# Four graph layers on one core: the adjacency's transpose by block loads and a VectorE transpose, and layer 2's last product kept in PSUM

## The chip, the cores and the metric

The kernel runs on one core of one Trainium2 chip. The core has five engines that run side by side, each through its own queue and in order: TensorE (PE, with its weight loads as PEld), VectorE (DVE), ScalarE (ACT), GpSimd (POOL) and SyncE (SP, which here issues nearly all transfers). [...] The metric is the device time of one execution in microseconds (us); lower is better. A line number such as L997 is a line of the kernel before.

## The reference

The input is x, 64 graphs of 256 nodes with 256 features, and adj, a 256 x 256 matrix of weights for each graph. Four layers follow each other, each as x = layernorm(x + layer(x, adj)). Layer 0 is a recurrence over the nodes. The change lies in layers 1 to 3:

```python
# layer 1: normalized adjacency times a linear map
degree = adj.sum(-1); d = degree ** -0.5            # 0 where the degree is 0
out1 = relu((adj * d[:, :, None] * d[:, None, :]) @ (x @ W.T + b))
# layer 2: attention with one head, masked by adj
att = softmax(scores * adj - 9e15 * (1 - adj), axis=2)
out2 = relu((att @ v) @ Wo + bo)
# layer 3: attention with 8 heads of 32 features
scores = where(adj > 0, q @ k.T / sqrt(32), -9e15)
out3 = (softmax(scores) @ v) @ Wo + bo
```

## The kernel before, in words

`_recurrence` computes layer 0 node by node, for all graphs at once. `_layers` then does layers 1 to 3 graph by graph. Each graph is an object of class `Graph`, and each of its methods is one step. Rows and columns of a 256 x 256 matrix lie as [128 partitions, 2 halves, 256].

The order of work is written out by hand. `ROUND` (L1246) lists the steps of one round, and the loop at L1257 runs rounds t = -1 to 66. In one round five graphs are at work, each in another part of its way: L (graph t+1) adds the residual of layer 0, takes degrees and prepares adj; A (graph t) is in layer 1; B (t-1) in layer 2; C (t-2) and E (t-3) in layer 3. The schedule is manual, so every engine runs its part of the steps in the order of this list. A round begins with graph t+2's loads. A graph's loads are thus issued about two rounds ahead of their use; SP also has the two stores of a round in its queue (L1162 and L1242).

These steps matter for the change:

- `load` (L1030): three transfers of 256 KB from SP: xin (x), ad (adj, in its own layout) and y (layer 0's result).
- `adT` (L1065), the step L.adT near the end of a round. PE transposes ad by four 128 x 128 transposes against an identity into one PSUM bank (`flipped`, L982). ACT copies it out in two halves, scaled by the degrees' roots: adT, which layer 1 uses one round later (`g`, L1086). DVE makes neg3 from the same bank: 0 where the transposed adj is above 0, and -9e15 elsewhere. Layer 3 adds neg3 to its transposed scores (L1190).
- `xT` (L1076): PE transposes the normalized x of a graph, and ACT copies it to SBUF. The next round begins with A.xT.1 and B.xT.2, right behind L.adT.
- `s3` (L1171): layer 3's scores for four heads; DVE adds neg3 (L1190), ACT takes the exponential (L1191), and POOL adds the two halves of each head's result to p3s (L1193), from which PE makes the softmax's sums.
- `o3` (L1197): PE multiplies p3s by ones (L1207) and p by v (L1216). In the program it stands behind the two xT; behind it comes `qk2` (L1100), PE's product of the weights with B's xT.
- `f2` (L1141), the end of layer 2. PE's product pm lies in PSUM; DVE scales it by 1/sums and adds a bias row, half by half, into an SBUF tile f (L1145), and then does y = max(f, 0) + y (L1149).

The PSUM banks with the tag "mm" (L966) are four, handed round among all products and transposes of these steps.

Of the kernel before, what the change touches and what calls it, by code (L numbers as in the profile page):

```python
# [9 lines left out]
F32 = mybir.dt.float32  # L10
BF16 = mybir.dt.bfloat16
AF = mybir.ActivationFunctionType
ALU = mybir.AluOpType
AX = mybir.AxisListType

NEG = 9000000000000000.0
# [3 lines left out]
P = 128  # L20
# [891 lines left out]
def _layers(tc, ident, Hd, Yd, x, adj, weights, out):  # L912
# [8 lines left out]
    nc = tc.nc  # L921
    nat, W2, W3, b1_r, b2_r, b3_r, cols = weights
# [6 lines left out]
    with ExitStack() as ctx:  # L929
# [9 lines left out]
        io = ctx.enter_context(tc.tile_pool(name="l_io", bufs=3))  # L939
# [26 lines left out]
        def bank(name, shape=(P, 2, D)):  # L966
            return ps.tile(list(shape), F32, tag="mm", name=name, bufs=4)

        for c in range(2):
            pt = bank(f"w1_{c}", (P, 2, P))  # L970
# [11 lines left out]
        def flipped(src, t):  # L982

            pt = bank(f"tr_{t}")
            for a in range(2):
                for c in range(2):
                    nc.tensor.transpose(
                        pt[:, a, c * P:(c + 1) * P], src[:, c, a * P:(a + 1) * P], ident
                    )
            return pt  # L990

        def product(lhsT, rhs, t):

            pm = bank(f"mm_{t}")
            for c in range(2):
                for k in range(2):
                    nc.tensor.matmul(  # L997
                        pm[:, c, :], lhsT[:, k, c * P:(c + 1) * P], rhs[:, k, :],
                        start=(k == 0), stop=(k == 1),
                    )  # L1000
            return pm

        def new(tag, t, bufs=2, shape=(P, 2, D)):
            return work.tile(list(shape), F32, tag=tag, name=f"{tag}_{t}", bufs=bufs)
# [17 lines left out]
        class Graph:  # L1022
# [7 lines left out]
            def load(self):  # L1030
                b = self.b
                self.xin = io.tile([P, 2, D], F32, tag="xin", name=f"xin_{b}")
                nc.sync.dma_start(self.xin, x[b].rearrange("(c p) d -> p c d", p=P))
                self.ad = io.tile([P, 2, N], F32, tag="ad", name=f"ad_{b}", bufs=4)
                nc.sync.dma_start(self.ad, adj[b].rearrange("(c p) m -> p c m", p=P))
                self.y = io.tile([P, 2, D], F32, tag="y", name=f"y_{b}", bufs=7)
                nc.sync.dma_start(self.y, Hd[:, b, :].rearrange("(c p) d -> p c d", p=P))

# [24 lines left out]
                nc.vector.tensor_mul(self.dis, self.dis, self.some)  # L1063

            def adT(self):  # L1065
                pt = flipped(self.ad, f"ad_{self.b}")
                self.adT_sb = new("adT", self.b)
                for c in range(2):
                    nc.scalar.activation(
                        self.adT_sb[:, c, :], pt[:, c, :], AF.Copy, scale=self.dis[:, c:c + 1]  # L1070
                    )

                self.neg3 = new("neg3", self.b, 4)
                nc.vector.tensor_scalar(self.neg3, pt, 0.0, -NEG, ALU.is_le, ALU.mult)

            def xT(self, l):  # L1076
                pt = flipped(self.y, f"x{l}_{self.b}")
# [62 lines left out]

            def f2(self):  # L1141
                pm = product(self.pT2_sb, self.w2_sb, f"2f_{self.b}")
                f = new("f2", self.b)
                for c in range(2):
                    nc.vector.scalar_tensor_tensor(  # L1145
                        f[:, c, :], pm[:, c, :], self.sums2[:, c:c + 1], b2_r,
                        ALU.mult, ALU.add,
                    )
                nc.vector.scalar_tensor_tensor(self.y, f, 0.0, self.y, ALU.max, ALU.add)  # L1149


            def qk3(self, s):
# [104 lines left out]
        for t in range(-1, B + 3):  # L1257
            if 0 <= t + 2 < B:
                graphs[t + 2].load()
            for step in ROUND:  # L1260
                who, name, *args = step.split(".")
                b = t - "LABCE".index(who) + 1
# [213 lines left out]
```

## Time and profile before

| what | value |
|---|---|
| median of 3 runs | 3432.68 us (3432.17 to 3434.24) |
| the profiled execution | 3433.69 us |
| its span, first to last instruction | 3431.9 us |
| granted TensorE clock over the span | 0.980 |
| first ad load of layers 1 to 3 | at 1525.41 us |
| chain that ended last, by engine | PE 73%, DMA 9%, DVE 6%, SP's queue 3%, POOL 3%, ACT 2% |

The first 1524 us of the span are layer 0; the rest is layers 1 to 3. Busy time in the second part, 1600 to 3300 us, is the steady part of the rounds. The timeline gives start, length, engine, line, operation, out<-in, shapes and count; names there leave out numbers, so tr_ad is the bank of adj's transpose, mm the product of xT with weights, and neg stands for neg2 and neg3. In the slices of the page, each digit is a fortieth of the span, in tenths of busy time.

### The profile page before, as it was taken

Reading aid. Unit: us, or ns where it says so; the run is one execution under the profiler, and the core shown is the slowest. Engines: PE = TensorE matmul, PEld = TensorE weight load, DVE = VectorE, ACT = ScalarE, POOL = GpSimd, SP = SyncE. Lnnn points to the kernel's source line nnn. Section 1 sums busy time; section 2 is a strip of 40 time slices with the busy share of each in tenths; the row PEclk is TensorE's granted clock in tenths of the full one; section 3 lists DMA queues with packets and bytes.
Section 4 is the critical chain, followed back from the end, with each engine's and each line's share of the span. In section 5 each row is a group of like instructions: output and inputs, shape, how many; then the busy total and the mean of one; then the engine's idle time right before and its main releaser. Section 6 shows DMA issues by size and latency. Waiting matters only on the chain.

```text
span 3431.9 us, 79587 instructions
## 1 busy us (share of the span) xinstructions
PE 3219.7 (94%) x29350; PEld 2339.7 (68%) x29350; DVE 2480.2 (72%) x7061; ACT 1827.7 (53%) x4754; POOL 1871.0 (55%) x2165
## 2 busy tenths in 40 slices
PE   5799999999889998978999999999999999999997
PEld 4565555555445555547888888888888888888885
DVE  3476777766567777755888888888888888888875
ACT  0254454444444444435666666666666666666664
POOL 2376777676667777733444444444444444444443
PEclk8999999999999999999999999999999999999998
DMA  9756675788777575230111111111111111111100
GB/s 301 226 159 143 164 188 155 168 188 211 186 185 173 146 183 157 60 97 22 47 47 47 47 47 47 47 47 47 47 47 47 47 47 47 47 47 47 47 29 19
DMA packets 389341, 347.83 MB, mean 101 GB/s; under 512 B 107356, under 2 KB 355304, under 8 KB 383720
## 3 DMA queue, kind: packets, MB, share of 16 engines
q1 hardware_dynamic: 371256, 325.82, 35.3%
q10 hardware_dynamic: 17696, 16.91, 1.5%
q8 instruction: 234, 3.83, 0.5%
q14 instruction: 155, 1.27, 0.1%
HBM read 224.01 MB, written 99.61 MB: 94 GB/s over the span
## 4 chain that ended last, share of the span: by engine, by line
PE 73%; DMA 9%; DVE 6%; SPq 3%; POOL 3%; issue 3%; ACT 2%; ACTq 0%; POOLq 0%; DVEq 0%
PE mm L997 13%; PE rc L604 5%; PE rc L596 4%; PE s L1181 4%; PE mm_2f L997 3%; DVE ACC L629 3%; PE mm_3v L997 3%; PE mm_t L997 3%; PE mm_3f L997 3%; PE mm_2v L997 3%; PE mm_g L997 3%; PE mm_2s L997 3%; PE mm_2w L997 3%; PE o L1216 3%; PE late L520 3%
## 5 line engine op out<-in xcount | busy, mean ns | idle before, releaser
L629 DVE SCALAR_TENSOR_TENSOR ACC<-keep,S,ACC 128x128 f32<-128x128 f32 x1712 | 481.3, 344 | 256.5 <-ACT hs L647 228.1
L1193 POOL TENSOR_TENSOR p3s<-p 128x256 f32<-128x256 f32 x512 | 386.8, 786 | 366.8 <-ACT p L1191 366.5
L997 PE MATMUL mm<-xT,weights 128*128 128x256 f32 x2048 | 481.9, 383 | 2.8 <-ACT xT L1079 2.8
L997 PEld LDWEIGHTS mm<-xT,weights 128*128 128x128 f32 x2048 | 384.9, 190 | 79.3 <-issue 25.5
L1190 DVE TENSOR_TENSOR p<-s,neg 128x512 f32<-128x512 f32 x512 | 317.6, 682 | 115.3 <-PE s L1181 115.3
L666 POOL TENSOR_TENSOR ACC<-ACC,far 128x384 f32<-128x384 f32 (+1 forms) x313 | 372.6, 1190 | 24.6
L662 POOL TENSOR_TENSOR far<-hs,S 128x384 f32<-128x384 f32 (+1 forms) x313 | 304.2, 972 | 4.7
L961 ACT ACTIVATE y<-y,shift,rstd 128x256 f32<-128x256 f32 x512 | 273.4, 599 | 48.1 <-DVE shift L959 44.4
L1191 ACT ACTIVATE p<-p 128x512 f32<-128x512 f32 x512 | 295.3, 628 | 1.9 <-DVE p L1190 1.6
L803 POOL TENSOR_TENSOR ready<-ACC,dinv 128x128 f32<-128x128 f32 x255 | 101.7, 399 | 325.8 <-DVE ACC L629 325.8
L596 PE MATMUL rc<-WxT,xqT 128*64 128x256 f32 x2048 | 268.1, 382 | 0.6 <-issue 0.6
L1104 ACT ACTIVATE qk<-mm,weights 128x256 f32<-128x256 f32 x256 | 107.3, 470 | 269.6 <-PE mm L997 269.6
L613 ACT COPY xpT<-xpT_ps 128x128 f32<-128x128 f32 x256 | 68.1, 266 | 302.5 <-PE xpT_ps L611 302.5
L1093 POOL TENSOR_TENSOR y<-y,g 128x512 f32<-128x512 f32 x64 | 81.0, 1265 | 266.2 <-issue 266.2
L604 PE MATMUL rc<-WhT,rT 128*64 128x128 f32 x2048 | 170.2, 287 | 58.0 <-DVE rT L826 56.0
L1230 DVE RECIPROCAL rT<-o 128x256 f32<-128x256 f32 x128 | 223.7, 1748 | 0.3 <-PE o L1207 0.2
L953 POOL TENSOR_TENSOR rstd<-rstd,mhalf 128x2 f32<-128x2 f32 x256 | 173.5, 695 | 83.2 <-DVE rstd L952 81.5
L949 DVE BATCH_NORM_STATS2 st<-y 128x6 f32<-128x256 f32 x512 | 208.8, 408 | 10.5 <-POOL y L1093 9.8
L604 PEld LDWEIGHTS rc<-WhT,rT 128*64 128x64 f32 x2048 | 107.8, 137 | 158.1 <-DVE rT L826 137.0
L1058 POOL TENSOR_TENSOR dis<-dis,mhalf 128x2 f32<-128x2 f32 x64 | 44.8, 700 | 277.5 <-DVE dis L1057 260.7
L604 PE MATMUL rc<-WhT,xpT 128*64 128x128 f32 x2048 | 170.5, 288 | 26.7 <-ACT xpT L613 25.4
L604 PEld LDWEIGHTS rc<-WhT,xpT 128*64 128x64 f32 x2048 | 107.9, 137 | 115.3 <-ACT xpT L613 64.9
(161 smaller groups left out, 7378.5 us busy)
## 6 DMA issues: line engine op xcount, KB each, us to landing
xX<-in_x_dram ACTq DMA_DIRECT2D x16, 1024.0 KB
Us<-xu SPq DMA_DIRECT2D x64, 256.0 KB
xq<-in_x_dram SPq DMA_DIRECT2D x64, 256.0 KB
ACC<-Us SPq DMA_DIRECT2D x32, 512.0 KB
Es<-eu SPq DMA_DIRECT2D x64, 256.0 KB
early_sb<-Es SPq DMA_DIRECT2D x32, 512.0 KB
xin<-in_x_dram SPq DMA_DIRECT2D x64, 256.0 KB
ad<-in_adj_dram SPq DMA_DIRECT2D x64, 256.0 KB
```

The source lines that it names most:

```text
L596: nc.tensor.matmul(G[o * B:(o + 1) * B], xqT[a, i // 2][:, i % 2, kc, h * B:(h + 1) * B], WxT[:, kc, o, gates], start=False, stop=False, s ...
L604: nc.tensor.matmul(G[o * B:(o + 1) * B], hT[:, kc * B:(kc + 1) * B], WhT[:, kc, o, g], start=False, stop=(kc == 1), skip_group_check=True,)
L629: nc.vector.scalar_tensor_tensor(acc[:, 0, :], keep[:, j % 2, :], s, acc[:, 0, :], ALU.mult, ALU.add)
L662: nc.gpsimd.tensor_mul(tmp[:, 0:count, :], hs.unsqueeze(1).to_broadcast(shape), s.unsqueeze(2).to_broadcast(shape),)
L666: nc.gpsimd.tensor_add(acc, acc, tmp[:, 0:count, :])
L949: nc.vector.bn_stats(st, y[:, c, :])
L961: nc.scalar.activation(y[:, c, :], y[:, c, :], AF.Identity, bias=shift[:, c:c + 1], scale=rstd[:, c:c + 1],)
L997: nc.tensor.matmul(pm[:, c, :], lhsT[:, k, c * P:(c + 1) * P], rhs[:, k, :], start=(k == 0), stop=(k == 1),)
L1190: nc.vector.tensor_add(p, s_ps[i], self.neg3)
L1191: nc.scalar.activation(p, p, AF.Exp, scale=ISQ)
L1193: nc.gpsimd.tensor_add(both, p[:, 0, :], p[:, 1, :])
L1230: nc.vector.reciprocal(rT, o_ps[:, 1, :])
```

## The change

adT no longer goes through PE and PSUM. SP loads adj a second time, in 32 x 32 blocks: az has, on partition 32 j + r, for each half a of the columns, the rows r of eight row blocks i, with the 32 columns that begin at 128 a + 32 j. One DVE transpose then turns every 32 x 32 block in place, which puts the blocks where the whole transpose has them. ad itself is still loaded, since degrees and layer 2's mask use it. Each graph thus has eight more transfers, each of 256 pieces of 128 bytes, issued between ad and y.

ACT now reads the transpose from SBUF for adT, and so does DVE for neg3. In f2, DVE writes its scaled product back into the product's own PSUM bank, and the last operation reads it from there; the SBUF tile f is gone. The order in `ROUND` is as before.

```diff
@@ load
                 nc.sync.dma_start(self.ad, adj[b].rearrange("(c p) m -> p c m", p=P))
+                self.az = io.tile([P, 2, 8, 32], F32, tag="az", name=f"az_{b}", bufs=3)
+                for j in range(4):
+                    for a in range(2):
+                        at = a * P + j * 32
+                        nc.sync.dma_start(
+                            self.az[j * 32:(j + 1) * 32, a],
+                            adj[b, :, at:at + 32].rearrange("(i r) c -> r i c", r=32),
+                        )
                 self.y = io.tile([P, 2, D], F32, tag="y", name=f"y_{b}", bufs=7)
@@ adT
-                pt = flipped(self.ad, f"ad_{self.b}")
+                turned = new("adTr", self.b)
+                nc.vector.transpose(
+                    turned.rearrange("p a m -> p (a m)"), self.az.rearrange("p a i c -> p (a i c)")
+                )
                 self.adT_sb = new("adT", self.b)
                 for c in range(2):
                     nc.scalar.activation(
-                        self.adT_sb[:, c, :], pt[:, c, :], AF.Copy, scale=self.dis[:, c:c + 1]
+                        self.adT_sb[:, c, :], turned[:, c, :], AF.Copy, scale=self.dis[:, c:c + 1]
                     )
                 self.neg3 = new("neg3", self.b, 4)
-                nc.vector.tensor_scalar(self.neg3, pt, 0.0, -NEG, ALU.is_le, ALU.mult)
+                nc.vector.tensor_scalar(self.neg3, turned, 0.0, -NEG, ALU.is_le, ALU.mult)
@@ f2
-                f = new("f2", self.b)
                 for c in range(2):
                     nc.vector.scalar_tensor_tensor(
-                        f[:, c, :], pm[:, c, :], self.sums2[:, c:c + 1], b2_r,
+                        pm[:, c, :], pm[:, c, :], self.sums2[:, c:c + 1], b2_r,
                         ALU.mult, ALU.add,
                     )
-                nc.vector.scalar_tensor_tensor(self.y, f, 0.0, self.y, ALU.max, ALU.add)
+                nc.vector.scalar_tensor_tensor(self.y, pm, 0.0, self.y, ALU.max, ALU.add)
```

## Prediction

> **What bounds the kernel now.** I read four views, in this order. First the page: busy time by engine and the slices of the span.
>
> ```profile
> PE 3219.7 (94%) x29350; PEld 2339.7 (68%) x29350; DVE 2480.2 (72%) x7061; ACT 1827.7 (53%) x4754; POOL 1871.0 (55%) x2165
> PE   5799999999889998978999999999999999999997
> DVE  3476777766567777755888888888888888888875
> ```
>
> The change touches only the last 22 or so of the 40 slices, where TensorE (PE) is at 9. The busy time in stretches says how full it is there (columns: stretch, its length, then busy time of PE, PEld, DVE, ACT, POOL, the granted clock, DMA share, GB/s):
>
> ```profile
> 1600.00:3300.00 1700.00, 1699.83 (x11557) 1372.32 (x11556) 1368.34 (x3359) 1082.66 (x2356) 810.45 (x1002) 1.00 0.14 46
> ```
>
> PE has no idle time on the page and runs at full clock; VectorE (DVE) is at 80%, ScalarE (ACT) at 64%. Rounds repeat every 28.83 us (the same step starts at 2207.25 and at 2236.08 in the chain of waits). This invites the sum "four transposes fewer, so much faster". The chain of waits, for one round, shows where they lie (start, length, what):
>
> ```profile
> 2207.25 1.92 PE mm_2f L997 x8
> 2209.17 0.44 PE tr_ad L987 x4
> 2209.61 0.87 PE tr_x L987 x8
> 2210.48 0.57 PE o L1207 x8
> 2211.05 1.73 PE o L1216 x32
> 2212.78 0.89 PE o L1207 x8
> 2213.67 1.92 PE mm L997 x8
> ```
>
> The reader is to see two things: the removed piece is 0.44 us a round, and right behind it PE works off products that other engines have only just fed. The second L1207 group takes 0.89 where the first takes 0.57, since it waits for POOL's p3s; and mm (layer 2's q) needs the second xT copy of ACT. So the timeline of those engines decides, in the same round:
>
> ```profile
> 2209.66 0.87 DVE L1145 SCALAR_TENSOR_TENSOR f<-mm_2f,sums,weights 128x256 f32<-128x256 f32 x2
> 2210.57 1.14 DVE L1149 SCALAR_TENSOR_TENSOR y<-f,y 128x512 f32<-128x512 f32 x1
> 2211.91 0.69 DVE L1074 TENSOR_SCALAR neg<-tr_ad 128x512 f32<-128x512 f32 x1 [0.20 <-ACT adT L1069]
> ```
>
> ```profile
> 2208.97 2.19 ACT L1191 ACTIVATE p<-p 128x512 f32<-128x512 f32 x4
> 2211.05 0.83 ACT L1069 ACTIVATE adT<-tr_ad,dis 128x256 f32<-128x256 f32 x2
> 2211.76 1.08 ACT L1079 COPY xT<-tr_x 128x512 f32<-128x512 f32 x2
> ```
>
> ACT does p, adT, xT without a gap; its second xT ends at 2212.84, and mm's record begins at 2213.60. So ACT leads by only 0.76 us, and adT stands in ACT's queue **ahead of** xT. Today adT waits for nobody: PE's tr_ad ended at 2209.61, ACT came to it at 2211.05.
>
> **The change, part by part.**
>
> *PE:* minus 0.44 us a round on the path. The built program has the four transposes gone and nothing else moved.
>
> *The new wait.* adT now needs DVE's transpose, which the built program puts behind p, the two f and y, and in front of neg3. Behind adT on ACT stand both xT copies; PE's mm waits for the second. Step by step:
> - The first f starts at 2209.66 as now and takes 0.47 (page's form: 474 ns), to 2210.13. Both f now write one PSUM tile, and in the built program the second waits for the first; now they overlap (0.87 for two). With the 0.04 us that such a wait costs (f ends 2210.53, y starts 2210.57) it runs 2210.17 to 2210.64.
> - y reads PSUM and one SBUF tile. The row like it is L1239 (688 ns for 512 elements); a SCALAR_TENSOR_TENSOR takes 50 ns more than a TENSOR_TENSOR (474 of L1145 against 424 of L1231). So 0.74: 2210.68 to 2211.42, against 2211.71 now. That is a gain of 0.4 on the op.
> - The transpose, 128x512 from SBUF, is in no row. From below: a copy of 256 elements SBUF to SBUF (L975) takes 0.28 where one from PSUM (L973) takes 0.42, two elements in the time of one; 512 would then take about 0.42. From above: the slow L1149, 1.12. Most 512-element rows lie at 0.68 to 0.69 (L1053, L1074, L1190), and I take 0.69. It starts 0.08 before y's end, as L949 does behind L1074 (2212.52 against 2212.60): 2211.34 to 2212.03.
> - Then 0.04 to ACT (as from DVE's shift to ACT's y). adT's source is now SBUF. Two PSUM-sourced ones follow each other at 0.36 (0.83 for two, 466 ns each); two of L961, SBUF-sourced, at 0.49 (599 each). I take 0.45, nearer to the latter: xT begins at 2212.07 + 0.90 = 2212.97.
> - Two xT take 1.08: 2214.05. PE follows 0.06 later (as mm_2f on pT): **2214.11 against 2213.60, +0.5 us a round.** PE waits here, and all 0.44 that it saved goes into the wait.
>
> [...]
>
> *neg3* comes from SBUF and behind the transpose. It lies on nobody's path until the next rounds; DVE's next deadline is oT for mm_3f, ready at 2218.73 for a start at 2220.61, a cover of 1.9 us. It takes 0.42 to 0.69 and may have to wait for POOL:
>
> ```profile
> 2225.67 1.26 POOL L1093 TENSOR_TENSOR y<-y,g 128x512 f32<-128x512 f32 x1 [4.10 <-issue]
> 2225.68 1.27 DVE L952 TENSOR_SCALAR rstd<-mv 128x2 f32<-128x2 f32 x1
> ```
>
> A DVE operation on two columns takes 1.27 here and 0.17 elsewhere: it ends when POOL's does. y (1.14, two SBUF sources) beside POOL's p3s is the same sight, and one p3s of that group takes 1.18 where the others take 0.73. [...]
>
> *Loads.* Eight more transfers a graph: SP issues of this size take 0.44 plus 0.05, so 3.9 us a round between ad and y. SP has a gap of 7.4 us behind y (2210.32 to the Yd store at 2217.76), and y is used a round later (2243), so nothing waits. The packets of 128 B, 2048 a graph, take 13 ns in the median where layer 0 loads such ones; on 16 engines that is about 2 us of a round. DMA stands at a share of 0.14. At the start it shows: POOL's first residual waits for the first y ("8.31 <-DMA y"), and that y is issued 3.9 us later. I take +3 us, once, between 0 and 6.
>
> **Sum.** adT and a following round with steady traffic come in rounds 2 to 62, 61 times: 61 x 0.52 = 32, plus 3 = 35. The profiled execution took 3433.69 (span 3431.9 and 1.8 around it), 1.0 above the median of 3432.68. So 3434 + 35 = 3469 for it, and 3468 for a median. What a measurement can tell from no change is 0.2%, about 7 us.
>
> **Rivals.**
> - *The wait, as summed* (66%): the transpose 0.60 to 0.76, ACT's step 0.42 to 0.49, y 0.69 to 0.76, give +0.35 to +0.68 a round, +21 to +41, with the start 3455 to 3482.
> - *A short transpose* (8%): 0.42 takes 0.27 off the round: 61 x 0.25 + 3 = 18, 3451. For it: SBUF copies run so. Against: reductions and two-source ops do not.
> - *All prices at their low ends* (6%): also f overlapping as now (-0.12), y at 0.69 (-0.05), ACT at 0.36 (-0.18): -0.10 a round, -6 + 3, 3430, no difference.
> - *PE's saving arrives* (8%): 61 x 0.44 = 27, less 3: **3409**, faster. It decides once the second xT is ready by 2213.11, that is 0.94 us sooner than I sum; then p3s, 0.45 sooner by y's new source, holds PE no longer either. For it: PE is at 100%. Against: DVE reaches the transpose only behind y, in the order shown.
> - *A slow transpose or late loads* (12%): at 1.12, +0.43, and ACT at 0.49, +0.08: 61 x 1.03 + 3 = 66, 3499. For it: reads across blocks of 32 partitions are in no row here.
>
> That the change does not do what it says is excluded by the built program's order. Faster 0.09, the same 0.05, slower 0.86. Range 3444 to 3500: it leaves out the two lowest rivals and a little of the highest, 18% in all.
>
> **What the profile will show.** If right: no tr_ad, PE idle before mm with ACT xT as releaser, about 0.9 us a round; ACT idle before adT for about 1 us, released by DVE; a transpose of about 0.69; y near 0.74; rounds of 29.35 us. If the transpose is short, PE's wait shrinks to 0.6. If PE stays without a gap and rounds take 28.4, my order of ACT's work was wrong. A first round delayed by more than 6 us would mean that the loads cost more than I took.

## The result, and the profile after

| | before | after |
|---|---|---|
| median | 3432.68 us (5 runs, 3429.06 to 3434.24) | 3455.99 us (5 runs, 3453.47 to 3468.01) |
| ratio, 95% interval | 1 | 1.007 [1.0052, 1.0088] |
| the profiled execution (span) | 3433.69 us (3431.9) | 3467.47 us (3465.7) |
| a steady round in the trace | 28.84 us | 29.21 us |

The kernel became 23 us slower. The profiled execution of after lies 11.5 us above its median, so the two spans, 33.8 us apart, must be split before they are read. Layer 0, whose code is the same, ends at 1522.37 us in the trace of before and at 1528.31 in that of after; in the eight experiments below it ends anywhere from 1513.18 to 1523.62. These 5.9 us are no part of the change. From layer 0's end to the first mm_2s product the traces differ by 2.6 (43.27 and 45.88 us; e1 below, which has none of the new loads either, has 45.59, so this too varies). From the first mm_2s product to the last, which is all rounds, it is **25.2 us** (1814.23 and 1839.47). Of the 63 intervals between these products, 60 are steady rounds (all but the first two and the last). In each trace 57 or more of the 60 agree with their median within 0.02 us, so the length of a round is the finest measure in this study, and I use it beside the medians.

The page of after, the lines that answer to those shown of before:

```profile
PE 3199.9 (92%) x29094; PEld 2320.5 (67%) x29094; DVE 2497.6 (72%) x7125; ACT 1833.7 (53%) x4754; POOL 1842.6 (53%) x2165
PE   5799999999889998868999999999999999999998
DVE  3376767766667776745888888888888888888885
...
L997 PE MATMUL mm<-xT,weights 128*128 128x256 f32 x2048 | 485.8, 386 | 54.2 <-ACT xT L1091 54.2
```

In the steady rounds the slices show PE at 9 before and after, and tell nothing. The last line does: of 54.2 us that PE stood idle ahead of mm (2.8 before), all was released by ACT's xT. The busy time in the same stretch as before (columns: stretch, its length, busy time of PE, PEld, DVE, ACT, POOL, granted clock, DMA share, GB/s) says how much it is:

```profile
1600.00:3300.00 1700.00, 1653.04 (x11165) 1332.67 (x11164) 1367.22 (x3370) 1074.99 (x2325) 773.09 (x987) 1.00 0.20 55
```

PE has 47 us of gaps in 1700 where it had 0.2; the granted clock is 1.00 in both. POOL is 37 us less busy. Some 10 us of this are operations that no longer fall into the stretch (987 instead of 1002), since rounds are longer; the rest is that one p3s a round is shorter. The chain of waits, one round:

```profile
2202.28 0.70 DVE adTr L1076
2202.98 0.02 issue
2203.01 0.91 ACT adT L1081 x2
2203.92 0.96 ACT xT L1091 x2
2204.88 0.04 issue
2204.92 1.99 PE mm L997 x8
2206.92 1.73 PE mm_t L997 x8
```

tr_ad is gone from it; DVE's transpose, adT and xT now stand ahead of mm. The timeline of the engines, same round:

```profile
2200.62 1.01 DVE L1156 SCALAR_TENSOR_TENSOR mm_2f<-mm_2f,sums,weights 128x256 f32<-128x256 f32 x2
2200.64 2.81 POOL L1204 TENSOR_TENSOR p3s<-p 128x256 f32<-128x256 f32 x4 [2.88 <-ACT p L1202]
...
2201.66 0.69 DVE L1160 SCALAR_TENSOR_TENSOR y<-mm_2f,y 128x512 f32<-128x512 f32 x1
2202.27 0.70 DVE L1076 STREAM_TRANSPOSE adTr<-az 128x512 f32<-128x512 f32 x1
...
2203.01 0.91 ACT L1081 ACTIVATE adT<-adTr,dis 128x256 f32<-128x256 f32 x2 [0.95 <-DVE adTr L1076]
2203.01 0.72 DVE L1086 TENSOR_SCALAR neg<-adTr 128x512 f32<-128x512 f32 x1
...
2203.82 1.05 ACT L1091 COPY xT<-tr_x 128x512 f32<-128x512 f32 x2
...
2204.92 1.99 PE L997 MATMUL mm<-xT,weights 128*128 128x256 f32 x8 [0.81 <-ACT xT L1091]
```

ACT is idle for 0.95 us until the transpose ends, though what xT copies (tr_x) has lain ready in PSUM since about 2201; xT stands behind adT in ACT's order. PE waits 0.81 for it. From 1610 to 3300 us PE has a single wait in the list, and ACT has this one among others (columns: who waited for whom, us in total, times, longest):

```profile
PE mm L997 <- ACT xT L1091: 46.8, 58, 1.2
```

```profile
ACT adT L1081 <- DVE adTr L1076: 56.2, 58, 1.6
```

### The profile page after: what moved, and what is told of

Read it like the earlier page. It is cut to its first block, busy times and chain, and to the rows that moved or that the text cites. A ratio compares the mean times of both kernels' runs of the same rounds, so it can differ in the third digit from the quotient of the medians.

```text
span 3465.7 us, 79713 instructions
## 1 busy us (share of the span) xinstructions
PE 3199.9 (92%) x29094; PEld 2320.5 (67%) x29094; DVE 2497.6 (72%) x7125; ACT 1833.7 (53%) x4754; POOL 1842.6 (53%) x2165
## 4 chain that ended last, share of the span: by engine, by line
PE 55%; ACT 15%; DMA 13%; DVE 10%; issue 3%; SPq 3%; POOL 2%; ACTq 0%; DVEq 0%; POOLq 0%
PE mm L997 13%; PE rc L604 6%; DMA xin<-in_x_dram 4%; PE rc L596 4%; ACT p L1202 4%; DVE ACC L629 4%; PE mm_t L997 3%; PE mm_3f L997 3%; PE mm_2v L997 3%; PE mm_2s L997 3%; PE mm_g L997 3%; PE late L520 3%; PE z_ps L596 3%; ACT xT L1091 2%; ACT sm L1018 2%
## 5 line engine op out<-in xcount | busy, mean ns | idle before, releaser
L1204 POOL TENSOR_TENSOR p3s<-p 128x256 f32<-128x256 f32 x512 | 358.2, 731 | 365.9 <-ACT p L1202 365.9
L997 PE MATMUL mm<-xT,weights 128*128 128x256 f32 x2048 | 485.8, 386 | 54.2 <-ACT xT L1091 54.2
L961 ACT ACTIVATE y<-y,shift,rstd 128x256 f32<-128x256 f32 x512 | 273.4, 599 | 38.8 <-DVE shift L959 35.2
L604 PE MATMUL rc<-WhT,xpT 128*64 128x128 f32 x2048 | 171.0, 288 | 25.9 <-ACT xpT L613 25.4
```

Of the source, the lines that this page charges most:

```text
L604: nc.tensor.matmul(G[o * B:(o + 1) * B], hT[:, kc * B:(kc + 1) * B], WhT[:, kc, o, g], start=False, stop=(kc == 1), skip_group_check=True,)
L961: nc.scalar.activation(y[:, c, :], y[:, c, :], AF.Identity, bias=shift[:, c:c + 1], scale=rstd[:, c:c + 1],)
L997: nc.tensor.matmul(pm[:, c, :], lhsT[:, k, c * P:(c + 1) * P], rhs[:, k, :], start=(k == 0), stop=(k == 1),)
L1204: nc.gpsimd.tensor_add(both, p[:, 0, :], p[:, 1, :])
```

## The experiments

**Theory.** In-order ACT makes xT wait for adT, adT for the transpose, the transpose for y on DVE; that costs the round more than PE saves. **Rivals:** the loads cost the time; the transpose as such does (by its time on DVE, or by holding up POOL beside it); or f2's change does. The kernels undo or move one piece at a time. Each ratio is against runs of the kernel before in the same set (medians 3431.2 and 3431.48 us).

**e1: f2's part alone**, in the kernel before.

```diff
-                f = new("f2", self.b)
-                        f[:, c, :], pm[:, c, :], self.sums2[:, c:c + 1], b2_r,
+                        pm[:, c, :], pm[:, c, :], self.sums2[:, c:c + 1], b2_r,
-                nc.vector.scalar_tensor_tensor(self.y, f, 0.0, self.y, ALU.max, ALU.add)
+                nc.vector.scalar_tensor_tensor(self.y, pm, 0.0, self.y, ALU.max, ALU.add)
```

> Only layer 2's end changes; adj's transpose stays on PE. Theory (y with two SBUF sources takes turns with POOL's p3s): y falls from 1.15 to about 0.69, the p3s of 1.18 to 0.73, the last p3s of a round ends 0.45 earlier, PE reaches mm about 0.3 sooner: rounds of 28.5 us against 28.84, some 19 us less in all, about 3414. Rival (the end of layer 2 lies beside other work and is worth nothing): rounds of 28.84, no change.

Measured: 3405.65 us, ratio 0.9925 [0.9899, 0.995]; rounds of 28.39. From e1's timeline:

```profile
2223.41 2.81 POOL L1192 TENSOR_TENSOR p3s<-p 128x256 f32<-128x256 f32 x4 [2.93 <-ACT p L1190]
2224.38 0.69 DVE L1148 SCALAR_TENSOR_TENSOR y<-mm_2f,y 128x512 f32<-128x512 f32 x1
```

and from that of e2, where f2 is the old one:

```profile
2224.81 3.26 POOL L1205 TENSOR_TENSOR p3s<-p 128x256 f32<-128x256 f32 x4 [2.90 <-ACT p L1203]
2225.69 1.09 DVE L1161 SCALAR_TENSOR_TENSOR y<-f,y 128x512 f32<-128x512 f32 x1
```

With y read from PSUM, y takes 0.69 instead of 1.09 to 1.15, and the four p3s beside it take 2.81 instead of 3.26. The 0.45 us saved on POOL is the 0.45 us saved on the round: f2 is not the loss, it is a gain of 26 us. It is not the two SBUF sources alone that make y long. In the first round of before, POOL does nothing from 1570.25 to 1582.13, and the same y from f takes 0.69 there:

```profile
1579.27 0.69 DVE L1149 SCALAR_TENSOR_TENSOR y<-f,y 128x512 f32<-128x512 f32 x1
```

**e2: the other part alone**: after, with f2 as before.

```diff
+                f = new("f2", self.b)
-                        pm[:, c, :], pm[:, c, :], self.sums2[:, c:c + 1], b2_r,
+                        f[:, c, :], pm[:, c, :], self.sums2[:, c:c + 1], b2_r,
-                nc.vector.scalar_tensor_tensor(self.y, pm, 0.0, self.y, ALU.max, ALU.add)
+                nc.vector.scalar_tensor_tensor(self.y, f, 0.0, self.y, ALU.max, ALU.add)
```

> The changed kernel with layer 2's end as before. Theory (PE waits for xT, which stands on ACT behind adT, which waits for DVE's transpose behind y): y at 1.15 puts the transpose at 12.5 us after the round's first 2s product instead of 12.2, rounds of about 29.5 us, total 3475 to 3485. Rival (what costs are the eight loads or adT's reading from SBUF, not DVE's order): rounds as in the changed kernel, 29.2, total 3456.

Measured: 3468.97 us, ratio 1.0101 [1.008, 1.0123]; rounds of 29.47, so the transposition alone costs 0.63 a round. The total is 6 us below what I expected, the round as expected. ACT's wait for the transpose grew by 0.26 (1.21 here, 0.95 in after), just as y ends later (12.55 us behind the round's first mm_2s product, 12.29 in after):

```profile
2226.70 0.70 DVE L1076 STREAM_TRANSPOSE adTr<-az 128x512 f32<-128x512 f32 x1
2227.44 0.91 ACT L1081 ACTIVATE adT<-adTr,dis 128x256 f32<-128x256 f32 x2 [1.21 <-DVE adTr L1076]
2227.44 0.91 DVE L1086 TENSOR_SCALAR neg<-adTr 128x512 f32<-128x512 f32 x1
```

**e3: the transpose ahead of layer 3's second p's** on DVE, so that it is done long before ACT wants it; nothing else is moved.

```diff
+            def turn(self):
+                self.turned = new("adTr", self.b)
+                nc.vector.transpose(...)
+
             def adT(self):
-                turned = new("adTr", self.b)
-                nc.vector.transpose(...)
...
-            B.pT2 E.norm_b.3 E.store A.norm_b.1 C.s3.1 B.f2
+            B.pT2 E.norm_b.3 E.store A.norm_b.1 L.turn C.s3.1 B.f2
             L.adT B.norm_a.2
```

> The changed kernel with the DVE transpose alone moved ahead of the second group of layer 3's scores, where DVE is idle for 1.75 us. Theory: adT starts right behind ACT's last p, at 12.0 instead of 12.94; xT is ready at 13.9; PE then is held by POOL's last p3s, which ends at about 13.4: rounds of 28.3 us, total about 3405, faster than both. Rival (loads, SBUF traffic): rounds stay at 29.2 or at least above 28.84.

Measured: 3414.76 us, ratio 0.9957 [0.9935, 0.9978]; rounds of 28.52. The same transpose, taken off adT's wait, turns 0.37 a round lost into 0.32 gained: the loss was the wait. But 28.52 is above the 28.3 expected. Who is late next shows in the last p3s and in neg3, which now runs beside it:

```profile
2226.20 0.78 DVE L1087 TENSOR_SCALAR neg<-adTr 128x512 f32<-128x512 f32 x1
```

```profile
L1205 POOL TENSOR_TENSOR p3s<-p x7: 732/737/911, 2219.6 to 2226.6; 128x256 f32<-128x256 f32 x7
```

(durations in ns, least, median, greatest.) One p3s takes 911 ns, and it is the last one, the one that PE waits for.

**e5: e3 with neg3 too moved**, to right behind the early transpose, away from the last p3s.

```diff
             def turn(self):
                 ...
+                self.neg3 = new("neg3", self.b, 4)
+                nc.vector.tensor_scalar(self.neg3, self.turned, 0.0, -NEG, ALU.is_le, ALU.mult)
             def adT(self):
                 ...
-                self.neg3 = new("neg3", self.b, 4)
-                nc.vector.tensor_scalar(self.neg3, self.turned, 0.0, -NEG, ALU.is_le, ALU.mult)
```

> As e3_turn_early, with neg3 made right behind the transpose, ahead of the second group of scores. In e3 neg3 took 0.78 beside POOL's last p3s, which took 0.92 instead of 0.73, and rounds were 28.52 where e4 had 28.35. Theory (neg3 from SBUF takes turns with POOL): the last p3s is back at 0.73, rounds of 28.35 us, total about 10 less than e3. Rival (the 0.17 comes from adT on ACT ahead of xT): rounds stay at 28.52.

Measured: 3403.58 us, ratio 0.9926 [0.9902, 0.995]; rounds of 28.34, 0.18 less than e3. The same line of e5:

```profile
L1205 POOL TENSOR_TENSOR p3s<-p x7: 727/732/740, 2221.9 to 2228.9; 128x256 f32<-128x256 f32 x7
```

No p3s is stretched now; neg3, which takes 0.91 in its new place, delays nobody there.

**e4: the transpose left where after has it, but ACT's adT moved behind xT.** This cures the order on ACT instead of the time on DVE.

```diff
-            A.xT.1 B.xT.2 E.o3 E.d3.0 B.qk2.0 C.norm_b.2 E.d3.1
+            A.xT.1 B.xT.2 A.adT E.o3 E.d3.0 B.qk2.0 C.norm_b.2 E.d3.1
...
-            L.adT B.norm_a.2
+            L.turn B.norm_a.2
```

(turn holds the transpose and neg3, adT only ACT's two operations.)

> The changed kernel with the transpose where it is, and only ACT's two adT copies moved behind the next round's two xT copies. Theory: the wait for the transpose stays, but nothing that PE needs stands behind it; PE is held by POOL's last p3s: rounds of 28.3 us, total about 3405. Rival (DVE itself is the bound, by 0.4 us more work a round): rounds above 28.84.

Measured: **3399.0 us, ratio 0.9901 [0.9874, 0.9929]**; rounds of 28.345. ACT goes from p to xT without a wait, and adT comes where ACT has time:

```profile
2224.73 2.19 ACT L1203 ACTIVATE p<-p 128x512 f32<-128x512 f32 x4
2226.81 1.06 ACT L1092 COPY xT<-tr_x 128x512 f32<-128x512 f32 x2
2227.86 0.91 ACT L1085 ACTIVATE adT<-adTr,dis 128x256 f32<-128x256 f32 x2
```

Of after's 47 us of gaps in PE nothing is left (1689.86 busy of 1690). Among the waits of PE's weight loads that are left in this stretch is the one for p3s:

```profile
PEld o L1219 <- POOL p3s L1205: 16.7, 59, 0.6
```

**e8: e4 with the old f2**, to see what the four transposes are worth on PE once the wait is gone.

```diff
+                f = new("f2", self.b)
-                        pm[:, c, :], pm[:, c, :], self.sums2[:, c:c + 1], b2_r,
+                        f[:, c, :], pm[:, c, :], self.sums2[:, c:c + 1], b2_r,
-                nc.vector.scalar_tensor_tensor(self.y, pm, 0.0, self.y, ALU.max, ALU.add)
+                nc.vector.scalar_tensor_tensor(self.y, f, 0.0, self.y, ALU.max, ALU.add)
```

> As e4_adT_behind_xT, with layer 2's end as before: so PE has four transposes fewer and nobody waits for the transpose, but y still takes turns with POOL. Theory (PE's saving runs into POOL's last p3s, which ends at 13.83 as before): mm at about 14.44 against 14.49, rounds of 28.75 to 28.8 us, total within 5 us of before. Rival (PE's saving is worth its 0.44): rounds of 28.4, total some 25 us below before.

Measured: 3433.43 us, ratio 1.0006 [0.9991, 1.002]; rounds of 28.785 against 28.84 before. PE is relieved of 0.44 us a round and the round gains 0.06: **where p3s holds it, PE's saving does not arrive.**

**e6: the loads alone**: the kernel before, with az loaded and not read.

```diff
+                self.az = io.tile([P, 2, 8, 32], F32, tag="az", name=f"az_{b}", bufs=3)
+                for j in range(4):
+                    for a in range(2):
+                        at = a * P + j * 32
+                        nc.sync.dma_start(...)
                 self.y = io.tile([P, 2, D], F32, tag="y", name=f"y_{b}", bufs=7)
```

> The kernel before with the eight block loads a graph added, and nobody reads them. Theory (SP, queues and SBUF have room): rounds of 28.84 us as before; the first y comes about 2 us later, total 0 to 4 us above before. Rival (small pieces of 128 bytes disturb the engines or delay y): rounds above 28.9, total over 6 us above before.

Measured: 3431.46 us, ratio 1.0006 [0.9993, 1.0019]; rounds of 28.845. Eight more transfers a graph in pieces of 128 bytes cost nothing that can be measured, although the first residual on POOL comes 8.03 us after the first load instead of 6.10 (6.69 in e1, without these loads), as in after (8.08). Here, at a DMA share of 0.20 (0.14 in before), the smaller pieces have no price in time.

**What holds mm.** The median over 45 steady rounds of each trace, in us behind the round's first mm_2s product (xT: end of the second copy):

| kernel | last p3s ends | xT ends | mm starts | round |
|---|---|---|---|---|
| before | 13.88 | 13.73 | 14.49 | 28.84 |
| after | 13.37 | 14.80 | 14.86 | 29.21 |
| e1 | 13.44 | 13.72 | 14.04 | 28.39 |
| e2 | 13.83 | 15.06 | 15.12 | 29.47 |
| e3 | 13.56 | 13.74 | 14.17 | 28.52 |
| e4 | 13.38 | 12.94 | 13.99 | 28.345 |
| e5 | 13.38 | 13.74 | 13.98 | 28.34 |
| e6 | 13.89 | 13.73 | 14.49 | 28.845 |
| e8 | 13.83 | 12.94 | 14.43 | 28.785 |

In every row mm starts either 0.60 to 0.61 behind the last p3s or 0.05 to 0.06 behind xT, whichever is later, and the round is mm's start and 14.35 to 14.36. Between p3s and mm lie the last row sums (o of L1218), which PE does ahead of mm.

**e7: these sums behind mm**, on top of e4.

```diff
                 heads(1)
-                sums(1)
+                self.late_sums = sums
+
+            def o3b(self):
+                self.late_sums(1)
...
-            A.xT.1 B.xT.2 A.adT E.o3 E.d3.0 B.qk2.0 C.norm_b.2 E.d3.1
+            A.xT.1 B.xT.2 A.adT E.o3 E.d3.0 B.qk2.0 E.o3b C.norm_b.2 E.d3.1
```

> As e4_adT_behind_xT, with the second group of layer 3's sums (which waits for POOL's last p3s) moved on PE behind layer 2's q product. Theory (in e4 PE waits for that p3s, so its saved transposes bring only 0.05 against e1): mm starts at about 13.0 instead of 13.99, PE has no gap left, rounds of 27.95 to 28.1 us, total about 3380. Rival (PE is the bound in e4 too): rounds stay at 28.35.

Measured: 3399.07 us, ratio 0.9905 [0.988, 0.9929]; rounds of 28.28. The expectation failed: 0.065 a round came, not 0.25 to 0.4. mm does start at 13.15, and the chain of waits is PE without a gap:

```profile
2199.92 0.57 PE o L1219 x8
2200.49 1.73 PE o L1228 x32
2202.21 1.92 PE mm L997 x8
2204.14 0.57 PE o L1219 x8
2204.71 1.93 PE mm_t L997 x8
2206.63 1.73 PE mm L997 x8
```

mm_t takes 1.93 here and 1.73 in after's chain: a product of eight that follows o's matmuls on 32 columns takes 0.19 longer, and the moved sums give the round one such place more. After's PE timeline shows the same behind s, whose matmuls are on tiles of 32 x 128. Neighbours overlap there, so take each product from the end of the one before it to its own end: mm_3v, behind s, has 1.91, mm_2s and mm_2w, behind products of the full array, 1.73 and 1.74:

```profile
2189.64 0.59 PE L997 MATMUL mm<-xT,weights 128*128 128x256 f32 x2
2190.07 1.89 PE L997 MATMUL mm_2s<-qk,qk 128*128 128x256 f32 x8
2191.89 1.15 PE L1192 MATMUL s<-qk,qk 32*128 32x256 f32 x16
2192.96 1.99 PE L997 MATMUL mm_3v<-weights,xT 128*128 128x256 f32 x8
2194.80 1.89 PE L997 MATMUL mm_2w<-weights,vT 128*128 128x256 f32 x8
```

That explains 0.19 of the miss; the other 0.15 is that mm, which PE now reaches without a gap, starts at 13.15 and not at 13.0. The round bears it out: from mm's start to its end e7 takes 15.12 us where the other kernels take 14.36, and the 0.77 between them are the moved sums (0.57) and the 0.19 or 0.20. That this belongs to the change of tile size on PE is read from these patterns and was not tried by itself.

## Why the prediction was right, point by point

- **The new wait** was the cause and stood where the prediction put it: PE idle before mm with xT as releaser (0.81 us a round, 0.9 forecast), ACT idle before adT released by DVE (0.95, about 1 forecast). e3 and e4 take it away in two different ways, and the loss goes with it.
- **Its size was too large**: the round grew by 0.37, not 0.52. Term by term (measured against forecast, medians of the steady rounds): the second f waits for the first, and y starts 1.04 behind the first f's start (1.02, +0.02); y takes 0.69 (0.74, -0.05); the transpose starts 0.08 before y's end, as forecast, and takes 0.70 (0.69, +0.01; the bounds were 0.42 and 1.12); the two steps of adT on ACT take 0.41 and 0.40 (0.45 each, **-0.09**); two xT take 1.05 (1.08, -0.03); the two hand-overs, from the transpose to adT and from xT to mm, take 0.09 together (0.10, -0.01). The sum is -0.15, which is the whole difference. The largest mis-sized term is ACT's step, for which I followed the row of L961. One bound was also added up wrongly: the low ends of the first rival (0.60, 0.42 and 0.69) give +0.32 a round, not +0.35; the measured 0.37 lies above both.
- **The start** cost what was forecast and for another reason, so that the sizes agree is luck. The forecast put 3 us on the loads; e6 has them and loses nothing. What the trace of after has instead is the first interval between mm_2s products, 31.52 us instead of 28.26, with a wait in it that I had not foreseen:

```profile
1589.48 0.91 ACT L1081 ACTIVATE adT<-adTr,dis 128x256 f32<-128x256 f32 x2 [5.29 <-DVE adTr L1076]
1589.48 0.43 DVE L1086 TENSOR_SCALAR neg<-adTr 128x512 f32<-128x512 f32 x1
1590.29 1.05 ACT L1091 COPY xT<-tr_x 128x512 f32<-128x512 f32 x2
1591.39 2.69 PEld L997 LDWEIGHTS mm<-xT,weights 128*128 128x128 f32 x8 [3.04 <-ACT xT L1091]
1591.40 3.41 PE L997 MATMUL mm<-xT,weights 128*128 128x256 f32 x8 [2.75 <-ACT xT L1091]
```

  No graph is in layer 3 yet, so ACT has no p's to cover the way from mm_2f over f, y and the transpose to adT. e2 has this interval at 31.38, e3 and e4, without the wait, at 27.66 and 27.6.
- **The sum.** 60 steady rounds x 0.37 = 22.2, the first interval 3.3, the second 0.8, the last -0.5, and 0.4 less for single rounds that ran long in the one trace and not in the other: 25.4, against 25.2 read from the trace and 23.3 between the medians. The forecast of 35 had 61 x 0.52 and 3. That the profiled execution, 3467.47, came so near to the 3469 forecast for it is luck too: layer 0 took 5.9 us longer in it than in the execution before. The 3468 forecast for a median was 12 us too high.
- **neg3 and y** have no term in the forecast for what they do beside POOL, and that held for the kernel as changed: in after, p3s ends at 13.37 and xT at 14.80. The prediction has p3s 0.45 sooner by y's new source; that was the author's estimate, from before's 1.18 and 0.73, and it is e1's gain to the hundredth. So the change contains a gain of 0.45 that its own other half hides.
- **The rival "PE's saving arrives"** named the right deciding point: in e4 the second xT ends at 12.94, before p3s, and the round gains 0.495, near the rival's 0.44. But it is not PE's saving. e1 gains 0.45 without it, e8 gains 0.06 with it alone. Before the change, mm waited for p3s, not for PE's own queue. The prediction's reading, "PE has no idle time on the page", misled: the records of o include the wait for p3s (0.89 where the same eight take 0.57), which the prediction had seen, and yet it priced the rival by PE's busy time.
- **Slow transpose, short transpose, low ends**: the transpose at 0.70 excludes the first two. Of the low ends only y came (0.69); f did not overlap, and ACT's pitch stayed above 0.36 (0.41 and 0.40).

## What to carry to other kernels

On an engine that works in order, look not at what a moved operation costs but at what is queued behind it: adT is needed 10 us later, yet the wait in front of it held xT, which was needed at once, and moving two instructions behind xT made 1.007 into 0.990. A PE that is busy for 100% may still be waiting inside its records (here o's 0.89 where the same eight take 0.57); work taken off it is worth what the next gate (here POOL's last p3s) lets through, so find that gate before pricing the saving. And undo the halves of a change one by one: here one half cost 38 us and the other brought 26.

## What the runs showed of the hardware that was not expected

- **In these traces DVE's neg3, and y from two SBUF tiles, and POOL's p3s wait for each other inside their records.** neg3 from SBUF took 0.43 us at 1589.48, where POOL ran nothing. In steady rounds it ends 0.28 to 0.29 after the end of the p3s that runs when it starts: p3s 13.37 and neg3 13.66 in after, 13.83 and 14.11 in e2, 7.67 and 7.95 in e5, 12.69 and 12.98 in e3. So it is recorded as 0.72 to 0.91. In turn the next p3s, if there is one, is stretched (0.73 to 0.91 in e3; 0.73 to 1.18 beside y from two SBUF tiles in before). One figure fits all of these: y from two SBUF tiles ends 0.55 after the end of the p3s that runs when it starts, and the stretched p3s 0.59 after the end of y or neg3. Each operation that waits thus ends its own undisturbed length (0.43, 0.69, 0.73) less 0.14 after the one that it waits for. Why they wait is not shown.
- The transpose did not stretch p3s: in after it runs from 12.20 to 12.90 beside two p3s of 0.73 each. It takes 0.70 us for 128x512 in f32 (700 to 712 ns in 58 of them), as long as most of DVE's other operations on 512 elements.
- A product of eight matmuls on the full array takes 0.19 us more when it follows matmuls on tiles of 32 (1.92 against 1.73, in the median, at each such place of a steady round of before and e7).
